# Layer 0 of a four-layer attention network: the first-layer sums of two points in one VectorE operation, with interleaved rows

## The chip, the cores and the metric

The kernel runs on one core of a Trainium2 chip. The number that counts is the device time of one execution in microseconds (us). Three executions of the kernel before took 3349.29, 3350.77 and 3352.3 us, median 3350.77 us.

A core has these engines, each with its own instruction queue: TensorE (PE in the profile, with its weight loads listed as PEld), VectorE (DVE), ScalarE (ACT), GpSimd (POOL) and SyncE (SP). In this kernel SP and POOL mostly issue DMA transfers. Engines wait for one another by semaphores. All arithmetic is in fp32.

## The reference, cut to what matters

Four layers run on x of shape (2, 512, 32, 32). The change lies in layer 0, deformable attention with 8 heads and 8 groups. Each group looks at 64 positions that are computed from the data, and the attention bias is a small network of the distance between each of the 1024 queries and each of these positions:

```python
pos = grid_q[:, :, None, :] - grid_kv[:, None, :, :]
bias = jnp.sign(pos) * jnp.log1p(jnp.abs(pos))
bias = jax.nn.relu(bias @ cpb_w1 + cpb_b1)      # 2 -> 128
bias = jax.nn.relu(bias @ cpb_w2 + cpb_b2)      # 128 -> 128
bias = (bias @ cpb_w3 + cpb_b3).reshape(b, GROUPS, H * W, Hd * Wd)
sim = jnp.einsum('bhid,bhjd->bhij', qh, kh) + bias
attn = jax.nn.softmax(sim, axis=-1)
```

Layers 1 to 3 are self-attention layers. The change doesn't touch them.

## The kernel before, in words

Layer 0 (function layer0) treats pairs of heads: t counts 8 of them, 2 images times 4 pairs. A pair has 128 positions, called points: 2 groups times 64. For each point the network's first layer is needed for 128 hidden channels (the partitions) and 1024 queries (32 rows y times 32 columns x).

**Tables.** The two distances of a point depend on x alone and on y alone. So offsets(t) computes, for each point, 32 numbers for x and 32 for y, and stores them to DRAM (slog_d, L471). load_tabs reads 16 points at a time back, spread over all partitions (L573), and scale_tab multiplies them by the channel's weight (VectorE for the first tables, L585; ScalarE after that, L587). What is left of the first layer is relu(tx[x] + ty[y]).

**first(p), L599.** One VectorE operation per point adds a row of 32 numbers, repeated over y, to a column of 32, repeated over x, and clips at zero: 1024 columns. It goes to one of eleven places (ring): three tiles of their own (named h1..., shown as h in the profile) and eight pieces of the buffer wa, which holds weights of layer 2 in the beginning and is otherwise free here.

**second, L616 and L625.** A step i takes four points. The 128 output channels of the second layer are cut into four parts of 32. For each part, eight matmuls (two halves of 512 queries times four points) fill one tile z: point k occupies partitions 32k to 32k+31, and its weights are 32 columns of cpb_w2, so that four matmuls with four different points run in the PE array side by side. In the trace an fp32 matmul is two records, so that a step has 64 of them. There are three z tiles in PSUM, which other small results share. ScalarE turns z into h2 with a relu and a bias per part (L625). Parts 1 and 3, the odd parts, go to the pool h2q, which has three buffers; part 2 goes to h2b (three buffers), part 0 to pieces of the buffer bridge or to h2j.

**joined, L630.** VectorE adds part 1 to part 0, and part 3 to part 2, with the sign that the third layer's weights need. GpSimd then issues DMA transfers that add the joined halves to each other and fold groups of partitions (L927 to L937), and SyncE copies some of them together (L931). third (L645) multiplies by the third layer's weights into sim, 20 steps late; scores (L653) adds the product of queries and keys.

**Order.** Everything in layer0 keeps, on each engine, the order in which the program writes it (in_order). The loop over i = 0 to 255 writes, for the parts k = 0 to 3 of a step: a call of first for point 4i + 7 + k (seven points are written ahead of the loop: AHEAD), the matmuls and the relu of a part, the joining of parts 3 and 2 of the step before at k = 1, and the joining of parts 1 and 0 at k = 3. Between them a chain of generators (behind) is advanced once at k = 1 and once at k = 3: finish(t) takes the softmax of the pair before, offsets(t+2) computes later positions (its small convolution: ScalarE products at L408, VectorE reductions at L414; then the small matmul po at L441), and samples(t+1) takes keys and values (kvbd at L534, wy, wx, shift, kq, values).

A place of the ring is rewritten as soon as PE has read it; the wait for this is VectorE's. In the same way ScalarE waits for a free buffer of h2q or h2b, and PE for a free z.

Before the loop PE multiplies weights of layer 2 together (folds, L135) while the first tables are made; small_fold ends with a VectorE operation at L855, after which VectorE's first sum is queued.

Of the kernel before, what the change touches and what calls it, by code (L numbers as in the profile page):

```python
# [79 lines left out]
def kernel(ctx: ExitStack, tc: tile.TileContext, a: dict, out: bass.AP):  # L80
# [111 lines left out]
    def layer0(l0, fold_d, t2_b, o2_b):  # L192
# [3 lines left out]
        two = l0.enter_context(tc.tile_pool(name="att2", bufs=2))  # L196
        vop = l0.enter_context(tc.tile_pool(name="att_vo", bufs=NPAIR))
        h2b = l0.enter_context(tc.tile_pool(name="att_h2b", bufs=3))
        h2q = l0.enter_context(tc.tile_pool(name="att_h2q", bufs=3))
        h2p = cycle([bridge[:, k, :] for k in range(6)])  # L200
        h2j = cycle([bridge[:, 6, :], bridge[:, 7, :], *(one.tile([P, HW], F32, name=f"h2j{k}") for k in range(2))])
        dram = l0.enter_context(tc.tile_pool(name="l0dram", bufs=1, space=DRAM))
# [30 lines left out]
        cpb_w2 = one.tile([P, P], F32, name="cpb_w2")  # L233
        nc.sync.dma_start(out=cpb_w2, in_=a["cpb_w2"])

        ring = [one.tile([P, HW], F32, name=f"h1{k}") for k in range(3)]
        ring += [qkv2.rearrange("p k n -> p (k n)")[:, k * HW : (k + 1) * HW] for k in range(6)]
        ring += [proj2.rearrange("p k n -> p (k n)")[:, k * HW : (k + 1) * HW] for k in range(2)]
        vb2 = one.tile([P, CC], F32, name="vb2")
        with nc.allow_non_contiguous_dma("512 numbers"):  # L240
            nc.sync.dma_start(out=vb2, in_=a["vb"][1].rearrange("(k p) -> p k", p=P))
# [7 lines left out]
        kvbd = [one.tile([P, P], F32, name=f"kvbd{i}") for i in range(2)]  # L249
        for w in actbd + kvbd:  # L250
            nc.gpsimd.memset(w, 0.0)
        ones = one.tile([P, P], F32, name="ones")
        nc.gpsimd.memset(ones, 1.0)


        qws = one.tile([P, NPAIR, P], F32, name="qws")
# [28 lines left out]
            nc.vector.tensor_tensor(dst, dst, src, ALU.max)  # L285

        def bias_weights():
            sort = h2b.tile([P, 7, P], F32, name="sort", tag="h2")
            row, below, w2t = [sort[:, k, :] for k in range(3)]
            perm = sort[:, 3:, :].rearrange("p b (r u) -> p b r u", u=32)  # L290
            few = one.tile([P, 28], F32, name="few")
            minus = few[:, 0:1]
            nc.vector.scalar_tensor_tensor(minus, cs("py", 0), 32.0, cs("px"), ALU.mult, ALU.add)
# [88 lines left out]
        def offsets(t):  # L382
# [85 lines left out]
            nc.scalar.activation(pos, pos, AF.Ln, bias=1.0)  # L468
            yield
            nc.vector.tensor_mul(pos, pos, sgn)  # L470
            nc.sync.dma_start(out=slog_d[t].rearrange("x p i -> p x i"), in_=pos)  # L471
            tables.add(t)

        tables = set()
# [10 lines left out]
        def samples(t):  # L485
# [22 lines left out]
                )  # L508
            nc.vector.tensor_mul(wsum[:, 2:3], wsum[:, 0:1], wsum[:, 1:2])
            yield  # L510
            wx = one.tile([P, P], F32, name="wx")
            nc.scalar.activation(wx, gpb[:, 0, :], AF.Abs, bias=cs("px"))
            nc.scalar.activation(wx, wx, AF.Relu, bias=1.0, scale=-1.0)
            wy = one.tile([P, 8, P], F32, name="wy", tag="wy")
# [11 lines left out]
            accumulate(pk[:, 0, :], [(xt[:, k, :], wy[:, k, :]) for k in range(8)])  # L526
            accumulate(pk[:, 1, :], [(wsum[:, 2:3].to_broadcast([P, P]), ident)])
            yield
            shift = one.tile([P, P], F32, name="shift")
# [12 lines left out]
            kq = one.tile([P, P], F32, name="kq")  # L542
# [3 lines left out]
            values = one.tile([P, P], F32, name="values")  # L546
            nc.scalar.copy(values, pkv[:, 1, :])
            yield
            pvo = zt([P, HW], "pvo")
# [39 lines left out]
        def first(p):  # L589

            chunk, point = divmod(p, 16)
            if point == 0:
                tabs_of.pop(chunk - 1, None)
                if chunk + 1 < NT * NCH:
                    load_tabs(chunk + 1)
            tx, ty = tabs_of[chunk]
            h1 = ring[p % len(ring)]

            nc.vector._custom_dve(  # L599
                TENSOR_ADD_SAT,  # L600
                out=h1.rearrange("p (y x) -> p y x", x=W),
                in0=tx[:, point, :].unsqueeze(1).to_broadcast([P, H, W]),
                in1=ty[:, point, :].unsqueeze(2).to_broadcast([P, H, W]),
                s0=float(np.finfo(np.float32).max),
                s1=0.0,
            )
            return h1

        def second(i, h1s, part):

            z = zt([P, HW], "z")
            lo = BLOCK[part]
            for half in range(2):
                n = slice(half * HALF, (half + 1) * HALF)
                for point in range(4):
                    nc.tensor.matmul(  # L616
                        z[point * 32 : point * 32 + 32, n],
                        cpb_w2[:, lo : lo + 32],
                        h1s[point][:, n],
                        start=True,  # L620
                        stop=True,
                    )
            ring = h2q if part % 2 else h2b if part else h2j if i % (4 if i < LAST else 2) else h2p
            h2 = ring.tile([P, HW], F32, name="h2", tag="h2") if ring in (h2q, h2b) else next(ring)
            nc.scalar.activation(h2, z, AF.Relu, bias=b2h[:, part : part + 1])  # L625
            return h2
# [30 lines left out]
        def finish(t, sim):  # L657

            b, pr = divmod(t, NPAIR)
            if pr == 0:  # L660
                aTs[b] = one.tile([P, NPAIR, HW], F32, name="aT")
            simb = one.tile([P, HW], F32, name="simb", tag="simb")
            nc.scalar.activation(simb, sim, AF.Identity, bias=simbias[t])
            yield
            table(AF.Exp)
            pt = zt([P, 8, P], "pt")
            for i in range(8):
                nc.tensor.transpose(pt[:, i, :], simb[:, i * P : (i + 1) * P], ident)
# [5 lines left out]
            at = one.tile([P, 8, P], F32, name="at", tag="simb")  # L674
# [12 lines left out]
            yield  # L687
            pa = zt([P, 8, P], "pa")
            for i in range(8):
                nc.tensor.transpose(pa[:, i, :], at[:, i, :], ident)  # L690
            nc.scalar.copy(aTs[b][:, pr, :], pa.rearrange("p i j -> p (i j)"))
            yield
            if pr < NPAIR - 1:
                return
            for m in range(CC):
                pp = zt([P, HW], "pp")
                project_out(pp, b, m, range(NPAIR))
                add_out(b, m, slice(0, HW), pp)
                yield
# [17 lines left out]
        def finish_last(sim, eights, fours, right_sums, left_sums):  # L717
# [7 lines left out]
            simb = one.tile([P, HW], F32, name="simb", tag="simb")  # L725
# [158 lines left out]
        steps = NT * NR  # L884
        h1s, parts, joins, sim, w1s = {}, {}, {}, None, None
        behind = chain(small_steps, offsets(1), samples(0))
        AHEAD = 7

        for p in range(AHEAD):
            h1s[p] = first(p)  # L890
        late_loads()
        for i in range(steps):
            for k, part in enumerate((1, 0, 3, 2)):
                if i % 4 == 1 and k % 2 == 0 and i // 4 + 1 in tabs_of:
                    scale_tab(i // 4 + 1, k // 2)
                p = 4 * i + AHEAD + k
                if p < 4 * steps:
                    h1s[p] = first(p)
                due = i - 20
                if k == 1 and 0 <= due < LAST and due % 16 == 0:  # L900
                    t, r = divmod(due, NR)
# [1370 lines left out]
```

## Time and profile before

| what | value |
| --- | --- |
| median of three executions | 3350.77 us |
| profiled execution | 3353.46 us |
| its span, first to last instruction | 3351.7 us |
| mean granted TensorE clock | 0.998 |
| PE busy | 3323.8 us (99%) |
| DVE busy | 2673.0 us (80%) |
| ACT busy | 1805.5 us (54%) |
| POOL busy | 676.7 us (20%) |
| first z matmul of the loop | at 59.6 us |
| last z matmul of the loop | at 1981.6 us |
| L599, first layer's sums | 1024 times, 1216 ns each |
| L630, joinings | 512 times, 1276 to 1277 ns each |

The profile is of one execution. Busy time is the time in which an engine had an instruction under way; matmuls are pipelined, so that four z matmuls which start together are recorded as some 593 ns each, while the next four start about 427 ns after them. A row of a group gives line, engine, operation, output and inputs, how often, then busy time and the mean in ns. In the timeline and the lists of waits, "<-" names what ended an idle time. "issue" means that nothing which the profile shows was waited for. L599 is line 599 of the kernel before; the same statement has another number in the kernel after (L599 becomes L603, L616 becomes L623, L625 becomes L632, L630 becomes L637).

### The profile page before, as it was taken

The page shows a single profiled execution, that of the slowest core. Times are in us where ns is not written, and L with a number is a line of the kernel's source. Part 1 is how long each engine was busy: PE and PEld are TensorE (multiplying, and loading weights), DVE is VectorE, ACT ScalarE, POOL GpSimd, SP SyncE. Part 2 cuts the span into 40 slices and gives each one's busy share as a digit, 9 for nine tenths or more (in the row PEclk, how much of TensorE's full clock was granted, in tenths as well). Part 3 has the DMA queues.
Part 4 walks back from the last instruction along what each step waited for, and adds up shares of the span by engine and source line. Part 5 has one row for each costly group of instructions (what it writes and reads, how often), then busy time and mean ns, then how long its engine had stood idle before and what let it go on. Part 6 is the DMA issues. An engine that isn't in the chain of part 4 may idle for free.

```text
span 3351.7 us, 61808 instructions
## 1 busy us (share of the span) xinstructions
PE 3323.8 (99%) x24813; PEld 1611.7 (48%) x24813; DVE 2673.0 (80%) x3540; ACT 1805.5 (54%) x2774; POOL 676.7 (20%) x804
## 2 busy tenths in 40 slices
PE   9999999999999999999999999999999999999999
PEld 4333333332333332333333339999953443687777
DVE  6999999999999799999999976455446465665556
ACT  4866877877877577877877652122136245122221
POOL 0333333333333233333333310000000000000000
PEclk9999999999999999999999999999999999999999
DMA  5778787787787577787787751000100000000111
GB/s 166 157 161 166 153 168 156 152 166 153 158 167 155 103 162 155 159 169 152 158 166 157 161 135 58 14 8 14 52 0 14 26 29 20 7 7 3 30 32 36
DMA packets 142488, 343.97 MB, mean 103 GB/s; under 512 B 36464, under 2 KB 51440, under 8 KB 141424
## 3 DMA queue, kind: packets, MB, share of 16 engines
q0 software_dynamic: 68400, 231.26, 36.5%
q1 hardware_dynamic: 72496, 103.95, 10.7%
q8 instruction: 197, 3.23, 0.4%
q10 hardware_dynamic: 1296, 4.72, 0.4%
q14 instruction: 99, 0.81, 0.1%
HBM read 71.46 MB, written 10.83 MB: 25 GB/s over the span
## 4 chain that ended last, share of the span: by engine, by line
PE 82%; DVE 9%; issue 5%; DMA 2%; ACT 1%; POOL 1%; DVEq 0%; SPq 0%; POOLq 0%; ACTq 0%
PE z L616 38%; PE pma L135 6%; PE pw L1435 6%; PE pmb L135 5%; PE pmv L1435 4%; PE score L1614 3%; PE pv L1626 3%; DVE wa L599 3%; PE pm L1435 3%; PE score L1435 3%; PE pmt L1435 1%; PE ppr L1435 1%; DVE h L599 1%; DMA bridge<-h 1%; DVE bridge L630 1%
## 5 line engine op out<-in xcount | busy, mean ns | idle before, releaser
L616 PE MATMUL z<-wa,cpb_w 128*32 128x512 f32 x11904 | 1779.2, 593 | 5.8 <-ACT h L625 3.7
L625 ACT ACTIVATE h<-z,b2h 128x1024 f32<-128x1024 f32 x768 | 851.3, 1114 | 347.9 <-PE z L616 310.6
L616 PE MATMUL z<-h,cpb_w 128*32 128x512 f32 x4480 | 983.2, 593 | 1.6 <-ACT h L625 1.6
L616 PEld LDWEIGHTS z<-wa,cpb_w 128*32 128x32 f32 x11904 | 497.2, 110 | 888.2 <-issue 778.1
L599 DVE CUSTOM_DVE_ANT_1 wa<-tab,tab 128x1024 f32<-128x1024 f32 x744 | 878.1, 1216 | 1.3 <-PE z L616 1.1
L616 PEld LDWEIGHTS z<-h,cpb_w 128*32 128x32 f32 x4480 | 256.6, 110 | 328.6 <-issue 292.1
L599 DVE CUSTOM_DVE_ANT_1 h<-tab,tab 128x1024 f32<-128x1024 f32 x280 | 332.9, 1216 | 2.3 <-PE z L616 2.2
L630 DVE SCALAR_TENSOR_TENSOR h<-h,turn,h 128x1024 f32<-128x1024 f32 x256 | 326.8, 1276 | 4.3 <-ACT h L625 4.3
L625 ACT ACTIVATE bridge<-z,b2h 128x1024 f32<-128x1024 f32 x162 | 180.8, 1116 | 121.4 <-PE z L616 119.0
L927 POOL DMA_DIRECT2D bridge<-bridge x150 | 127.6, 850 | 547.2 <-DMA bridge<-h 510.5
L630 DVE SCALAR_TENSOR_TENSOR bridge<-bridge,turn,h 128x1024 f32<-128x1024 f32 x162 | 206.8, 1277 | 4.2 <-ACT bridge L625 4.2
L934 POOL DMA_DIRECT2D bridge<-h x161 | 163.4, 1015 | 213.2 <-DVE h L630 123.6
L1278 ACT COPY p<-pma 128x128 f32<-128x128 f32 x80 | 21.3, 266 | 334.7 <-PE pma L135 334.7
L1270 DVE TENSOR_TENSOR upper<-pma,p 128x256 f32<-128x256 f32 x80 | 33.7, 422 | 178.6 <-ACT p L1278 178.5
L1615 ACT ACTIVATE p<-score 128x512 f32<-128x512 f32 x256 | 130.0, 624 | 81.2 <-PE score L1614 79.6
L927 POOL DMA_DIRECT2D h2j<-h2j x90 | 76.2, 847 | 323.0 <-DMA h2j<-h 293.6
L1647 DVE TENSOR_TENSOR acc<-acc,p 128x1024 f32<-128x1024 f32 x96 | 111.0, 1217 | 19.4 <-ACT p L1615 19.3
L625 ACT ACTIVATE h2j<-z,b2h 128x1024 f32<-128x1024 f32 x94 | 105.0, 1117 | 37.9 <-PE z L616 37.3
L1614 PE MATMUL score<-q,k 64*128 64x512 f32 x512 | 120.7, 604 | 1.1 <-DVE gm L1191 1.1
L630 DVE SCALAR_TENSOR_TENSOR h2j<-h2j,turn,h 128x1024 f32<-128x1024 f32 x94 | 120.0, 1276 | 0.0
L1626 PE MATMUL pv<-p,vT 128*64 128x512 f32 x512 | 116.5, 598 | 0.0
L937 POOL DMA_DIRECT2D bridge<-h2j x90 | 111.9, 1244 | 2.6 <-issue 1.8
(458 smaller groups left out, 4379.8 us busy)
## 6 DMA issues: line engine op xcount, KB each, us to landing
bridge<-h POOLq DMA_DIRECT2D x161, 512.0 KB, 5.5
h2j<-h POOLq DMA_DIRECT2D x94, 512.0 KB, 5.9
bridge<-bridge POOLq DMA_DIRECT2D x159, 256.0 KB, 3.9
tab<-slog_d SPq DMA_DIRECT2D x128, 256.0 KB, 4.6
h2j<-h2j POOLq DMA_DIRECT2D x90, 256.0 KB, 3.2
bridge<-bridge POOLq DMA_DIRECT2D x150, 128.0 KB, 5.4
bridge<-bridge SPq DMA_DIRECT2D x90, 128.0 KB, 3.7
bridge<-h2j SPq DMA_DIRECT2D x90, 128.0 KB, 3.6
```

The source lines that it names most:

```text
L135: nc.tensor.matmul(pm, w, m, start=(k == 0), stop=(k == len(pairs) - 1))
L599: nc.vector._custom_dve(TENSOR_ADD_SAT, out=h1.rearrange("p (y x) -> p y x", x=W), in0=tx[:, point, :].unsqueeze(1).to_broadcast([P, H, W] ...
L616: nc.tensor.matmul(z[point * 32 : point * 32 + 32, n], cpb_w2[:, lo : lo + 32], h1s[point][:, n], start=True, stop=True,)
L625: nc.scalar.activation(h2, z, AF.Relu, bias=b2h[:, part : part + 1])
L630: nc.vector.scalar_tensor_tensor(h2, h2, turn[:, part // 2 : part // 2 + 1], parts.pop(part + 1), ALU.mult, ALU.add)
L927: nc.gpsimd.dma_start(out=own[0:P:2], in_=own[1:P:2], accum_op=ALU.add)
L934: nc.gpsimd.dma_start(out=joins[i - 1], in_=other, accum_op=ALU.add)
L937: nc.gpsimd.dma_start(out=joins[i - 3 - j][j:P:4], in_=joins.pop(i - 3)[2:P:4], accum_op=ALU.add)
L1435: nc.tensor.matmul(out, stationary(l, k), moving(r, k), start=start and k == 0, stop=k == nk - 1, skip_group_check=not start,)
L1614: nc.tensor.matmul(sc, ks[m][r, s * P : (s + 1) * P], qs[m][r, n], start=True, stop=True)
L1615: nc.scalar.activation(p[:, part], sc, AF.Exp, scale=64 ** -0.5)
L1626: nc.tensor.matmul(pv[half][part * 64 : part * 64 + 64], vt[s % 4][:, lo : lo + 64], lps[s, half][:, part, :], start=(s == 0), stop=(s == 7),)
```

## The change

first(p) now makes the sums of two points, p and p + 1, in one operation of 2048 columns. Their rows are interleaved in the result: row y of the first point, then row y of the second, then row y + 1 of the first. Six double places make up the ring, room for twelve points, and eight points are written ahead of the loop. In a step the operation is written at k = 0 and k = 2. The matmuls of second read a point out of this: 16 runs of 32 words, 32 words apart.

For the operand ty the pair's 64 numbers have to lie as (y, point). The table in DRAM is stored in that order: the x half of slog_d is one DMA as before, the y half is two DMAs in which each number is a run of its own, 2048 numbers each.

The odd parts' pool h2q gets a fourth buffer. To make room, ones becomes a part of the tile sort and is set by VectorE, and some tiles share a buffer: simb and at with wy, wx with values, shift with kq.

```diff
-        h2q = l0.enter_context(tc.tile_pool(name="att_h2q", bufs=3))
+        h2q = l0.enter_context(tc.tile_pool(name="att_h2q", bufs=4))
...
-        ring = [one.tile([P, HW], F32, name=f"h1{k}") for k in range(3)]
-        ring += [qkv2.rearrange("p k n -> p (k n)")[:, k * HW : (k + 1) * HW] for k in range(6)]
-        ring += [proj2.rearrange("p k n -> p (k n)")[:, k * HW : (k + 1) * HW] for k in range(2)]
+        ring = [one.tile([P, 2 * HW], F32, name=f"h1{k}") for k in range(2)]
+        ring += [qkv2.rearrange("p k n -> p (k n)")[:, k * 2 * HW : (k + 1) * 2 * HW] for k in range(3)]
+        ring.append(proj2.rearrange("p k n -> p (k n)"))
...
-        ones = one.tile([P, P], F32, name="ones")
-        nc.gpsimd.memset(ones, 1.0)
...
-            sort = h2b.tile([P, 7, P], F32, name="sort", tag="h2")
+            sort = h2b.tile([P, 8, P], F32, name="sort", tag="h2")
+            ones = sort[:, 7, :]
+            nc.vector.memset(ones, 1.0)
...
-            nc.sync.dma_start(out=slog_d[t].rearrange("x p i -> p x i"), in_=pos)
+            nc.sync.dma_start(out=slog_d[t, 0], in_=pos[:, 0, :])
+            pairs = slog_d[t, 1].rearrange("(a k) i -> a (k i)", k=2).rearrange("a (i k) -> k a i", k=2)
+            with nc.allow_non_contiguous_dma("4096 numbers"):
+                for k in range(2):
+                    nc.sync.dma_start(out=pairs[k], in_=pos[k:P:2, 1, :])
...
-            wx = one.tile([P, P], F32, name="wx")
+            wx = one.tile([P, P], F32, name="wx", tag="values")
...
-            tx, ty = tabs_of[chunk]
-            h1 = ring[p % len(ring)]
+            tx, ty = [tab[:, point : point + 2, :] for tab in tabs_of[chunk]]
+            h1 = ring[p // 2 % len(ring)].rearrange("p (y k x) -> p y k x", k=2, x=W)
 
             nc.vector._custom_dve(
                 TENSOR_ADD_SAT,
-                out=h1.rearrange("p (y x) -> p y x", x=W),
-                in0=tx[:, point, :].unsqueeze(1).to_broadcast([P, H, W]),
-                in1=ty[:, point, :].unsqueeze(2).to_broadcast([P, H, W]),
+                out=h1,
+                in0=tx.unsqueeze(1).to_broadcast([P, H, 2, W]),
+                in1=ty.rearrange("p k y -> p (k y)")
+                .rearrange("p (y k) -> p y k", k=2)
+                .unsqueeze(3)
+                .to_broadcast([P, H, 2, W]),
                 s0=float(np.finfo(np.float32).max),
                 s1=0.0,
             )
-            return h1
+            return [h1[:, :, k, :] for k in range(2)]
...
-                        h1s[point][:, n],
+                        h1s[point][:, half * 16 : half * 16 + 16, :],
...
-            simb = one.tile([P, HW], F32, name="simb", tag="simb")
+            simb = one.tile([P, HW], F32, name="simb", tag="wy")
...
-        AHEAD = 7
-
-        for p in range(AHEAD):
-            h1s[p] = first(p)
+        AHEAD = 8
+
+        for p in range(0, AHEAD, 2):
+            h1s[p], h1s[p + 1] = first(p)
...
                 p = 4 * i + AHEAD + k
-                if p < 4 * steps:
-                    h1s[p] = first(p)
+                if p < 4 * steps and k % 2 == 0:
+                    h1s[p], h1s[p + 1] = first(p)
```

The shared buffers of at, shift, kq and values are marked in the same way as those of wx and simb, by a tag.

More of the change, by code (lines that the diff above doesn't have):

```diff
@@ L287, in bias_weights @@
         def bias_weights():
[L288 removed]
+            sort = h2b.tile([P, 8, P], F32, name="sort", tag="h2")
+            ones = sort[:, 7, :]
+            nc.vector.memset(ones, 1.0)
             row, below, w2t = [sort[:, k, :] for k in range(3)]
[L290 removed]
+            perm = sort[:, 3:7, :].rearrange("p b (r u) -> p b r u", u=32)
             few = one.tile([P, 28], F32, name="few")
@@ L528, in samples @@
             yield
-            shift = one.tile([P, P], F32, name="shift")
+            shift = one.tile([P, P], F32, name="shift", tag="kq")
             nc.scalar.mul(shift, pk[:, 1, :], col("bn1_b", pr))
@@ L541, in samples @@
             nc.tensor.matmul(pkv[:, 1, :], bd["vw"][:, pr, :], kv, start=True, stop=True)
-            kq = one.tile([P, P], F32, name="kq")
+            kq = one.tile([P, P], F32, name="kq", tag="kq")
             nc.scalar.copy(kq, pkv[:, 0, :])
@@ L545, in samples @@
             nc.scalar.mul(kqs[t], pkv[:, 0, :], s1q[:, pr : pr + 1])
-            values = one.tile([P, P], F32, name="values")
+            values = one.tile([P, P], F32, name="values", tag="values")
             nc.scalar.copy(values, pkv[:, 1, :])
@@ L673, in finish @@
             yield
-            at = one.tile([P, 8, P], F32, name="at", tag="simb")
+            at = one.tile([P, 8, P], F32, name="at", tag="wy")
             atv = at.rearrange("p i (g j) -> p (i g) j", j=NJ)
@@ L724, in finish_last @@
             project_out(pps[0], b, 0, range(2))
-            simb = one.tile([P, HW], F32, name="simb", tag="simb")
+            simb = one.tile([P, HW], F32, name="simb", tag="wy")
             for half, n in enumerate(halves):
```

## The prediction

> **What bounds the kernel now.** I read the table of busy time by stretch first, over eight stretches of the attention loop of layer 0, then the list of waits inside that loop, then the timeline around one repeated wait, then the rows of single groups for prices. The table (microseconds, PE, PEld, DVE, ACT, POOL busy) has these rows; the last line sums 70 to 1980 us:
>
> ```profile
> 300.00:540.00 240.00, 238.94 (x2168) 75.63 (x2164) 234.53 (x215) 182.02 (x253) 83.84 (x97) 1.00 0.78 159
> ...
> 1020.00:1260.00 240.00, 239.58 (x1972) 77.02 (x1968) 212.67 (x196) 162.00 (x233) 74.82 (x87) 1.00 0.68 139
> ...
> sum 1910.00, PE 1901.06 PEld 597.72 DVE 1839.46 ACT 1405.93 POOL 650.69; mean PE 237.63 PEld 74.71 DVE 229.93 ACT 175.74 POOL 81.34
> ```
>
> Two engines are nearly full: DVE has 71 us free in 1910, PE 9. So TensorE is the bound, and whatever VectorE saves is worth at most those 9 us. That PE's busy time is real work and not slow work shows in the chain that ended last, asked over 100 to 470 us:
>
> ```profile
> 210.64 109.87 PE z L616 x1024
> ...
> 428.48 1.21 DVE bridge L630
> 429.77 1.12 ACT h L625
> 430.93 8.79 PE z L616 x80
> ```
>
> 1024 records in 109.87 us are 256 groups of four column blocks at 0.429 us. A step of the loop has 64 records: 6.87 us of PE. DVE's step is two of each half: sums of two points 2.35 us, one joining (L630). Starts of such pairs lie 3.47 us apart (426.12 and 429.59 below), so 6.94 us per step, 0.07 more than PE, before any other VectorE work. DVE falls behind, and catches up only where PE has other matmuls.
>
> The 9 us of PE are these waits (total, times, longest), and below them ScalarE's waits for VectorE in the same stretch:
>
> ```profile
> PE z L616 <- ACT h L625: 5.3, 10, 0.6
> PE z L616 <- DVE kvbd L534: 2.1, 2, 1.6
> PE sim L645 <- DMA bridge<-bridge: 1.5, 2, 1.3
> ...
> ACT h L625 <- DVE h L630: 9.0, 8, 1.3
> ACT h L625 <- DVE bridge L630: 7.0, 6, 1.4
> ```
>
> The timeline (start, duration) shows how one of the first kind arises:
>
> ```profile
> 426.12 2.35 DVE L599 CUSTOM_DVE_ANT_1 wa<-tab,tab 128x1024 f32<-128x1024 f32 x2
> ...
> 428.39 1.28 DVE L630 SCALAR_TENSOR_TENSOR bridge<-bridge,turn,h 128x1024 f32<-128x1024 f32 x1
> ...
> 429.77 2.12 ACT L625 ACTIVATE h<-z,b2h 128x1024 f32<-128x1024 f32 x2 [1.36 <-DVE bridge L630]
> ...
> 430.93 0.64 PE L616 MATMUL z<-wa,cpb_w 128*32 128x512 f32 x4 [0.52 <-ACT h L625]
> ```
>
> ScalarE waits 1.36 us until the late joining frees one of three odd-part buffers; then PE waits for ScalarE. This recurs at 668, 908, 1411 and 1649 us. The other five waits for ACT h (455, 693, 932, 1436, 1674 us) follow a run of ScalarE's own small operations with no VectorE wait ahead of them.
>
> **The change part by part.**
>
> *The paired sum.* 1024 operations of 1024 columns become 512 of 2048. One takes 1216 ns. VectorE rows of 512 and 1024 columns (L1717 at 692, L1647 at 1217 ns) give 1.03 ns a column, so a pair should take 1216 + 1024 x 1.03 = 2.27 us against 2.35: 0.08 saved, 512 times, 41 us of VectorE. DVE's step becomes 6.94 - 2 x 0.08 = 6.78 us, below PE's 6.87. Both operands keep their kind, runs of 64 repeated and words repeated 32 times, for which the present runs of 32 already cost nothing over a plain 1024-column operation (1216 against 1217 ns). On the path the 41 us are worth nothing themselves: PE's matmuls cover them.
>
> *Twelve points, eight ahead, a fourth odd buffer.* The last point of a step was written in the step before it; now it is a full step earlier. Counted from the release of its place, VectorE had 6.87 - 1.2 = 5.7 us of room for it; now the second pair ends 2.27 + 1.2 + 2.27 = 5.7 us after the release and is read two PE steps after it, so the room is 13.7 - 5.7 = 8.0 us. The fourth buffer lets ScalarE run two quarter steps, 3.4 us, further ahead of the joining; the waits of 1.36 us end inside that. By starts of matmuls each of the five stops costs 0.72 us over the normal spacing: 5 x 0.72 = 3.6 us, all taken as gone. What comes late next is ScalarE itself: its five own runs stay, 5 x 0.55 = 2.7 us. The waits for kvbd (1.63 and 0.42 us) are VectorE lag: by 177 us it has done some 34 pairs, 2.7 us earlier, less one sum more before the loop (1.1 us); I take 1.5 us of the 2.1. The waits of L645 for a DMA (1.29 and 0.21 us) follow from late joinings and from queues; bounds 0 and 1.5, I take 0.5.
>
> *TensorE reads every second row.* Its moving operand becomes 16 runs of 32 words with as many skipped. Bounds come from three rows; in the first the code reads single words four apart, in the second two runs of 256, in the third 512 in one run:
>
> ```profile
> L1752 PE MATMUL pb<-proj,vb x8: 1047/1090/1339, 2621.5 to 2622.7; 128*32 128x512 f32 x8
> ...
> L1898 PE MATMUL den<-acc,ones x16: 592/604/617, 2940.4 to 3119.5; 128*32 128x512 f32 x16
> ...
> L616 PE MATMUL z<-wa,cpb_w x11904: 589/592/617, 59.6 to 1981.6; 128*32 128x512 f32 x199
> ```
>
> At worst a hop costs what it costs between single words, (1090 - 592) / 512 = 0.97 ns: 15 hops in 4096 groups are 60 us. At best nothing; a gain is excluded, since the same columns stream. Runs of 32 are nearer to runs of 256 than to single words, and L343, whose moving operand also has runs of 32, takes 275 ns like its contiguous neighbours of 128 columns. I take 0.
>
> The Trainium skill, page "Advanced Engine Details and Errata", section "Memory Cachelines", speaks against the edit in one line, that any non-contiguous access pattern slows matmuls significantly, and for it in another, that SBUF needs two hits on a 16-byte line. The first stands under PSUM, and by it the sum would move to the 60 us end; by the second it stays at 0, and L1752, one hit a line, is the slow row under both.
>
> *The y table written interleaved.* One store of 32 KB (L471) becomes one of 16 KB and two of 2048 single numbers, eight times; SP issues three instructions for one (0.36 to 1.3 us each) and is held at the y load until they land; the folded weights' stores queue behind. The first table is on the path. Its rows:
>
> ```profile
> 44.18 0.48 DVE L585 TENSOR_SCALAR tab<-tab,pc 128x512 f32<-128x512 f32 x1 [0.33 <-DMA tab<-slog_d]
> ...
> 52.70 0.16 DVE L855 TENSOR_TENSOR o_b<-pb,pc 128x4 f32<-128x4 f32 x1 [8.04 <-PE pb L135]
> ...
> 59.57 0.63 PE L616 MATMUL z<-h,cpb_w 128*32 128x512 f32 x3
> ...
> vb<-in_vb SPq DMA_DIRECT2D x1, 6.0 KB, 5.2
> ...
> d<-few SPq DMA_DIRECT2D x8, 2.0 KB, 1.4
> ```
>
> VectorE idles 8 us behind the table, and PE, busy with the folds until 59.6, needs two pairs (4.5 us) by then: the table may come by 55.1, 10.4 us late, for nothing. A load of 1536 single numbers lands in 5.2 us; all of it charged per number, 4096 take 13.9 us, 3.5 over the slack. The other end is nothing: a load of 512 such numbers took 5.1 us, so most is fixed. The far end is a store: 2 KB in 128 runs lands in 1.4 us (d<-few), all charged per run 45 us, 34 past the slack. I take 0, since the loads have runs of the same size. Later tables are needed some 100 us after their store; there the stores only share queue and engines with the join's transfers (L931, L937; median 3.7 and 5.7 us), bounds 0 and 1 us each, seven times; I take 0.5 in all.
>
> The page "DMA: Bandwidth & Descriptors", section "Specifications", says that below 512 B the engine does a read-modify-write. By that the stores would lie toward the far end; no row here stores single numbers to DRAM.
>
> *The rest*, all 0: ones is set by VectorE while it idles 2.79 us for prow at 15.7 us; shared buffers for wx and values, shift and kq, simb, at and wy follow one another in the same queues with matmuls between them. Cover gone, each would cost one ScalarE operation, about 1 us, per pair of heads.
>
> **Sum** against the profiled execution (3353.46 us, of which the span is 3351.7): -3.6 - 1.5 - 0.5 + 0.5 = -5.1, so 3348.4. That execution lies 2.7 us above the median 3350.77; on the median's scale 3345.7.
>
> **Rivals.**
>
> *All of PE's idle time goes* (30%): ScalarE's own runs are absorbed too, because it no longer enters them late. The list of waits allows 9 us: 3341.9. Against it: ScalarE had caught up (it waits 0.60 us for PE at 449.15) before the stop at 454.78.
>
> *Nothing goes* (8%): joinings stay late by something else, for instance if a pair takes 2.35 us or more. DVE's step is then again over PE's: 3351.
>
> *Slower: the hop is paid* (10%). Place: all 16384 matmuls of L616. Price: 4096 x 15 x c. From c = 0.08 ns the gain is gone, from 0.19 ns the kernel is slower by over 0.2%; at 0.97 ns 3406. Against it, L1898 and L343.
>
> *Slower: the single-number stores* (8%). At 45 us for the first table PE stands idle 34 us at 59.6 us: 3380; from 22 us to landing it decides. What is left (4%) is a joining chain that stops PE several times a head pair, 3358.
>
> **How the numbers follow.** 0.2% is 6.7 us, about what a measurement of this kernel can tell from no change. The forecast, a gain of 3 to 6.7 us, has 40%; with the 8% of nothing, same is 0.48; faster is 0.30; slower 0.10 + 0.08 + 0.04 = 0.22. The likeliest case's own range is 3344 to 3348. The range goes from 3340 (all idle time and two microseconds of spread between runs) to 3362, which takes in small prices of hop or store and leaves out their far ends.
>
> **What would show it.** L603, the sum's new line: 512 operations of 2.27 us; 2.43 or more would break the first step. The z matmuls stay at 592 ns, a group at 0.429 us; 600 or more shows the hop. ScalarE's waits for L637, the joining, fall from 21 us to under 5; PE's for ACT h from ten to five. DVE's idle time ahead of sums and joinings grows from about 12 to some 40 us, for it now waits for PE. The first z still starts near 59.6 us. I am wrong if PE's stops stay with VectorE 41 us lighter, or if z slows.

## The result, and the profile after

The kernel after takes 3440.78 us, median of six executions (3431.93 to 3446.95), against 3350.67 us of the kernel before on the same chip (six, 3348.89 to 3352.3). The ratio is 1.0269, with a 95% interval of 1.0257 to 1.0281: slower by 90 us. The profiled execution took 3440.16 us, its span is 3438.4 us, and its mean granted TensorE clock 0.988 where it was 0.998.

The page of the kernel after, busy time of each engine:

```profile
span 3438.4 us, 61019 instructions
...
PE 3347.4 (97%) x24813; PEld 1637.0 (48%) x24813; DVE 2640.2 (77%) x3029; ACT 1803.6 (52%) x2774; POOL 676.0 (20%) x803
```

VectorE is lighter by 33 us (2673.0 before; 41 were forecast), and yet the span is longer by 86.7 us; 83.3 of these are there when the last z matmul starts (2064.9 us, before 1981.6). The same table by stretch as in the prediction (PE, PEld, DVE, ACT, POOL busy, then granted clock, share of the DMA engines, GB/s), kernel after:

```profile
300.00:540.00 240.00, 231.15 (x2077) 80.48 (x2072) 220.14 (x144) 174.46 (x245) 81.16 (x94) 0.98 0.84 153
...
1020.00:1260.00 240.00, 235.08 (x1918) 74.00 (x1914) 202.63 (x129) 153.83 (x209) 75.25 (x88) 0.99 0.69 138
...
sum 1910.00, PE 1843.21 PEld 599.82 DVE 1739.71 ACT 1352.57 POOL 630.38; mean PE 230.40 PEld 74.98 DVE 217.46 ACT 169.07 POOL 78.80
```

PE now stands idle for 67 us of these 1910, where it was 9, and no other engine has taken over as the bound: VectorE has 170 us free, where it was 71. The list of waits of PE in the loop (total, times, longest), kernel after:

```profile
PE z L623 <- ACT h2j L632: 38.0, 6, 9.9
PE pk L135 <- ACT h2j L632: 11.1, 1, 11.1
PE sim L652 <- DMA bridge<-bridge: 7.2, 4, 4.4
PE z L623 <- ACT h L632: 5.6, 6, 2.9
PE z L623 <- DVE h L603: 4.6, 2, 4.4
PE pk L135 <- ACT bridge L632: 3.5, 1, 3.5
PE z L623 <- ACT bridge L632: 1.5, 2, 0.9
```

They add up to 71.5 us, 62.6 more than before. Few waits, and long: one or two for each pair of heads, the largest those that end at 183.9, 494.1, 743.8, 990.6, 1521.5 and 1767.4 us. The waits on which the forecast gain rested, two for kvbd and five behind the joining at the small matmul po, are gone; each of the six new stops costs more than all of those together. The timeline around the second stop, kernel after (start, duration):

```profile
465.92 0.33 SPq L471 DMA_DIRECT2D slog_d<-pos  x1
...
466.29 3.33 SPq L475 DMA_DIRECT2D slog_d<-pos  x2
...
469.15 0.86 POOL L934 DMA_DIRECT2D h2j<-h2j  x1 [3.56 <-DMA h2j<-h]
...
471.02 0.86 POOL L941 DMA_DIRECT2D bridge<-h  x1 [1.01 <-issue]
...
490.07 0.50 SPq L938 DMA_DIRECT2D bridge<-h2j  x1
...
491.51 0.86 POOL L934 DMA_DIRECT2D bridge<-bridge  x1 [18.78 <-DMA bridge<-h]
...
492.89 1.11 ACT L632 ACTIVATE h2j<-z,b2h 128x1024 f32<-128x1024 f32 x1 [11.02 <-issue]
...
494.05 2.79 PE L623 MATMUL z<-wa,cpb_w 128*32 128x512 f32 x12 [8.31 <-ACT h2j L632]
```

Read from the end. PE waits 8.3 us for a z tile that ScalarE has not emptied; ScalarE waits 11 us to write h2j ("issue" in the timeline; what it waits for follows from the kernel's order). Part 0 goes to four places in turn, two called h2j and two in bridge; out of the place that is due, SyncE's copy (L938) has still to read, and that copy goes out only at 490.07, since it needs the fold of h2j that GpSimd had issued at 469.15. GpSimd in turn waits 18.8 us for the transfer which it issued at 471.02. Both transfers were issued 3 to 5 us behind the two stores of single numbers (L475, issued in 466.29 to 469.62). The chain of work that ended last, asked over 480 to 500 us, says the same:

```profile
471.02 20.21 DMA bridge<-h
491.23 0.28 issue
491.51 0.56 POOL bridge L934
492.07 8.10 DMA bridge<-h
```

The median of such a transfer was 5.5 us before; this one takes 20.2. Now the stretches around it, as in the table above; first the kernel after, then the same part of the pair of heads in the kernel before:

```profile
470.00:484.00 14.00, 13.45 (x128) 3.91 (x124) 14.00 (x10) 10.67 (x20) 1.72 (x3) 1.00 1.57 29
484.00:494.00 10.00, 1.75 (x20) 0.26 (x8) 2.36 (x2) 1.11 (x2) 1.75 (x2) 0.70 0.89 151
494.00:499.00 5.00, 4.95 (x28) 1.24 (x32) 4.02 (x3) 4.07 (x4) 1.65 (x2) 0.57 1.08 256
```

```profile
452.00:466.00 14.00, 13.45 (x132) 3.94 (x128) 14.00 (x14) 12.24 (x25) 5.17 (x6) 1.00 0.94 224
```

For 14 us the DMA engines move 29 GB/s instead of 224, although packets are under way all the time (share 1.57: two queues' packets are open at once, SyncE's with a share of 0.78 and GpSimd's with 0.77). Nothing is lost on PE yet in this stretch (13.45 us busy in both); PE stops from 485.7 on. Then comes a second price: when PE starts again its granted clock is 0.57 in the mean of the next 5 us, and L623's longest matmul takes 1063 ns where it was 617. There are ten such stretches of half clock in the loop of after, 3.4 to 10.2 us each with the idle time in them, and none before. Counted by the starts in the trace, 39 groups of matmuls come some 0.85 us apart instead of 0.43, which is 17 us, and two runs of pk matmuls come 0.21 us apart instead of 0.11, which is 3.6 us. So 62.6 us of waits and some 21 us of slow clock make up the 83.3 us to within a few us; smaller terms on both sides I have not traced.

The page "TensorE: Matmul & The Clock Gate" of the Trainium skill, section "What's actually happening", says that an idle window of about 3.4 us halves TensorE's clock, until it has been busy for about as long. The granted clock of 0.57 behind a stop of 8.3 us agrees with it. The stop of 2.9 us that ends at 1285.8 us is shorter than that and still has half clock behind it (0.50 from 1286.8 to 1290.2 us); one of 2.2 us that ends at 2072.3 us has not (1.00).

The start of the loop, timeline of the kernel after:

```profile
37.89 18.16 SPq L577 DMA_DIRECT2D tab<-slog_d  x2
...
55.88 0.55 DVE L589 TENSOR_SCALAR tab<-tab,pc 128x512 f32<-128x512 f32 x1 [14.86 <-DMA tab<-slog_d]
...
59.12 0.49 DVE L589 TENSOR_SCALAR tab<-tab,pc 128x512 f32<-128x512 f32 x1 [2.69 <-DMA tab<-slog_d]
...
59.64 4.49 DVE L603 CUSTOM_DVE_ANT_1 h<-tab,tab 128x2048 f32<-128x2048 f32 x2
...
62.08 1.92 PE L623 MATMUL z<-h,cpb_w 128*32 128x512 f32 x4 [4.39 <-DVE h L603]
```

The first tables are ready at 59.6 instead of 44.7 us, 15 us later, and the first z comes 2.5 us later than before, after a stop of 4.4 us. Last, the rows of the two parts that were meant to change, kernel after (min, median and max in the second):

```profile
L603 DVE CUSTOM_DVE_ANT_1 wa<-tab,tab 128x2048 f32<-128x2048 f32 x340 | 776.6, 2285 | 3.0 <-PE z L623 2.6
```

```profile
L623 PE MATMUL z<-wa,cpb_w x10880: 592/592/1063, 75.1 to 2058.1; 128*32 128x512 f32 x198
```

A pair's sum takes 2.285 us, and a z matmul that reads every second row still takes 592 ns.

### The profile page after: what moved, and what is told of

Its sections match the earlier page's. It is cut to its first block, busy times and chain, and to the rows that moved or that the text cites. A ratio compares the mean times of both kernels' runs of the same rounds, so it can differ in the third digit from the quotient of the medians.

```text
span 3438.4 us, 61019 instructions
## 1 busy us (share of the span) xinstructions
PE 3347.4 (97%) x24813; PEld 1637.0 (48%) x24813; DVE 2640.2 (77%) x3029; ACT 1803.6 (52%) x2774; POOL 676.0 (20%) x803
## 4 chain that ended last, share of the span: by engine, by line
PE 73%; DMA 10%; DVE 7%; issue 7%; POOL 2%; ACT 1%; SPq 1%; DVEq 0%; POOLq 0%; ACTq 0%
PE z L623 32%; PE pma L135 6%; PE pw L1442 6%; DMA bridge<-h 5%; PE pmb L135 5%; PE pmv L1442 4%; PE score L1621 3%; PE pv L1633 3%; PE pm L1442 3%; PE score L1442 3%; DVE wa L603 2%; DMA bridge<-bridge 2%; PE ppr L1442 1%; DMA h2j<-h 1%; DVE h L637 1%
## 5 line engine op out<-in xcount | busy, mean ns | idle before, releaser
L623 PE MATMUL z<-wa,cpb_w 128*32 128x512 f32 x10880 | 1203.3, 596 | 33.1 <-ACT h2j L632 26.5
L603 DVE CUSTOM_DVE_ANT_1 wa<-tab,tab 128x2048 f32<-128x2048 f32 x340 | 776.6, 2285 | 3.0 <-PE z L623 2.6
L623 PEld LDWEIGHTS z<-wa,cpb_w 128*32 128x32 f32 x10880 | 364.3, 110 | 831.6 <-issue 697.2
L623 PE MATMUL z<-h,cpb_w 128*32 128x512 f32 x5504 | 618.5, 597 | 16.6 <-ACT h2j L632 11.4
L603 DVE CUSTOM_DVE_ANT_1 h<-tab,tab 128x2048 f32<-128x2048 f32 x172 | 392.9, 2285 | 1.4 <-PE z L623 1.2
L623 PEld LDWEIGHTS z<-h,cpb_w 128*32 128x32 f32 x5504 | 184.4, 110 | 422.3 <-issue 361.9
```

Of the source, the lines that this page charges most:

```text
L603: nc.vector._custom_dve(TENSOR_ADD_SAT, out=h1, in0=tx.unsqueeze(1).to_broadcast([P, H, 2, W]), in1=ty.rearrange("p k y -> p (k y)") .rear ...
L623: nc.tensor.matmul(z[point * 32 : point * 32 + 32, n], cpb_w2[:, lo : lo + 32], h1s[point][:, half * 16 : half * 16 + 16, :], start=True, ...
```

## Experiments: is it the stores?

Theory S: the two stores of 2048 single numbers hold up the transfers of the joining, and cost the 90 us. Rival P: something else in the change does, the ring of pairs, the matmuls' operand or the buffers that now share a place.

**The stores alone.** The kernel before, with the two stores of after and nothing else; a sum of one point reads its column two words apart.

```diff
-            nc.sync.dma_start(out=slog_d[t].rearrange("x p i -> p x i"), in_=pos)
+            nc.sync.dma_start(out=slog_d[t, 0], in_=pos[:, 0, :])
+            ...
+                for k in range(2):
+                    nc.sync.dma_start(out=pairs[k], in_=pos[k:P:2, 1, :])
...
```

> The kernel before with nothing changed but the store of the y table: two DMAs of 2048 single numbers, and the sum reads the column two words apart. Theory S: the whole loss is here, 3437 us (3425 to 3450), with the stops at the same places, and TensorE's clock halved after them. Rival P: within 0.2% of before, 3344 to 3357.

Measured: 3450.75 us (3447.52 to 3454.33) against 3349.93, ratio 1.03 (1.0283 to 1.0318). So the stores alone cost 101 us, somewhat more than S expected, and more than the whole change; by that the rest of the change would give about 10 us back. (The sum that reads words two apart takes 1218 ns against 1216, so it is not the sum.) The long waits of PE are there again:

```profile
PE z L624 <- ACT h2j L633: 47.3, 5, 13.4
PE z L624 <- ACT h L633: 21.7, 13, 8.8
```

**Half the numbers, waited for by nothing.** The kernel before, with one extra store of 2048 single numbers per pair of heads, into a DRAM tile that nobody reads. It tells whether the price is the traffic or the wait for the table.

```diff
+        spare_d = dram.tile([NT, P // 2, 64], F32, name="spare_d")
...
+            pairs = spare_d[t].rearrange("a (i k) -> k a i", k=2)
...
+                nc.sync.dma_start(out=pairs[0], in_=pos[0:P:2, 1, :])
```

> The kernel before with one spare DMA of 2048 single numbers per pair of heads to a scratch piece of DRAM, half of what the kernel after stores, and nothing that waits for it. Theory S in its plain form, that each number costs PE its share: 90 x 7/8 / 2 = 39 us, 3390 us. Theory S with room in the buffers (the engines are held for about half of 18 us, and the joining chain has some 7 us of room): 0 to 20 us, 3351 to 3371 us. Rival P: 3351 us.

Measured: 3394.97 us, ratio 1.0132 (1.0112 to 1.0152), 45 us more. Nothing waits for this store, so the price is what it does to the other transfers, and half of the numbers cost half.

**The same runs, not to DRAM.** Both stores of 2048 numbers, as extra work, from SBUF to a tile in SBUF.

```diff
+        spare_s = one.tile([P // 2, 64], F32, name="spare_s")
...
+            pairs = spare_s.rearrange("a (i k) -> k a i", k=2)
...
+                for k in range(2):
+                    nc.sync.dma_start(out=pairs[k], in_=pos[k:P:2, 1, :])
```

> The kernel before with two spare DMAs of 2048 single numbers per pair of heads that go from SBUF to SBUF, as many runs of as few bytes as in the kernel after, but no write to DRAM. If it is the number of runs that holds the engines: 3420 to 3440 us. If it is the writing of single numbers to DRAM: within 0.2% of before, 3344 to 3357 us.

Measured: 3350.11 us, ratio 1.0 (0.999 to 1.0009). In the 14 us behind the stores the DMA engines move 174 GB/s here, against 224 in the kernel before (table by stretch), so these stores are not free for them; but PE is as busy as before:

```profile
450.00:464.00 14.00, 13.45 (x132) 3.97 (x128) 14.00 (x14) 12.13 (x25) 4.32 (x5) 1.00 0.99 174
```

So it is not the number of runs, nor SyncE's time to issue them, nor the reading of single numbers from SBUF. It is writing them to DRAM, in this dense layout; the runs on other layouts follow below.

## Experiments: what is the rest of the change worth?

**The table stored whole.** The kernel after, with the store of before; the numbers of two points are interleaved later, in SBUF, by the operation that scales the y table anyway and now writes into a tile of its own. To make room, actbd, kvbd and the y table as it is loaded have one buffer each, and sums3 shares kq's.

```diff
-            nc.sync.dma_start(out=slog_d[t, 0], in_=pos[:, 0, :])
-            ...
+            nc.sync.dma_start(out=slog_d[t].rearrange("x p i -> p x i"), in_=pos)
...
+            if ax:
+                tabs_of[c][1] = two.tile([P, 16, 32], F32, name="taby")
+                dst = tabs_of[c][1].rearrange("p a y -> p (a y)").rearrange("p (a y k) -> p a k y", k=2, y=32)
+                tab = tab.rearrange("p (a k) y -> p a k y", k=2)
...
...
-                nc.scalar.activation(tab, tab, AF.Identity, bias=0.0 if ax else col("cpb_b1"), scale=w)
+                nc.scalar.activation(dst, tab, AF.Identity, bias=0.0 if ax else col("cpb_b1"), scale=w)
```

> The kernel after, with the table stored in one piece as before; the scaling that follows the load interleaves the y table into a tile of its own (room for it: one buffer each instead of two for actbd and kvbd, and sums3 shares kq's). The kernel before with single-number stores lost 100 us, the kernel after 90; so the rest of the change is worth 10 us: 3340 us (3336 to 3347). PE's waits in the loop fall from 9 us to under 4, z stays at 592 ns. Rival (the pairs help only where PE stands still for another reason, and give nothing without the stores): 3350 us within 0.2%. Rival (ScalarE's odd writes, up to 0.7 us a table, lengthen its runs): 3350 to 3357.

Measured: 3343.59 us (3340.41 to 3345.44) against 3350.78, ratio 0.998 (0.9971 to 0.9989): faster than the kernel before by 7.2 us. PE's waits in the loop:

```profile
PE z L624 <- ACT h L633: 3.0, 5, 0.6
PE sim L653 <- DMA bridge<-h: 2.1, 1, 2.1
```

The second lies behind the last z matmul (1968.5 us). In the loop 3.0 of the 8.9 us are left, five waits of 0.6 us that follow a run of ScalarE's own small operations, as at 451.4, 687.7 and 923.9 us. The pair's sum takes 2284 ns, the scaling of the y table 796 ns and that of the x table, still in place, 805: writing it interleaved costs nothing. More came out of the loop than these waits. From the first z matmul to the last it is 1909.8 us, where it was 1922.0, and the largest part of that lies in the matmuls of third, whose row took 35.6 us of busy time and 1.5 of waits before (first line, 60 to 1967 us) and takes 30.4 and no wait now (second line):

```profile
L645 PE MATMUL sim<-bridge,w 128*32 128x512 f32 x256 | 35.6, 594 | 1.5 <-DMA bridge<-bridge 1.5
```

```profile
L653 PE MATMUL sim<-bridge,w 128*32 128x512 f32 x256 | 30.4, 592 | 0.0
```

These 6.7 us, with 2.1 for kvbd and 2.3 for ACT h, are 11.1 of the 12.2; the wait of 2.1 us behind the last z takes some of it back.

**With three odd buffers.** The same kernel with the pool h2q as before.

```diff
-        h2q = l0.enter_context(tc.tile_pool(name="att_h2q", bufs=4))
+        h2q = l0.enter_context(tc.tile_pool(name="att_h2q", bufs=3))
```

> The run above with three odd-part buffers instead of four. If the waits for the joining at the small matmul po end by the lighter VectorE alone: as the run above, within 1 us. If they end by the fourth buffer, as the prediction has it: 3 to 4 us more than the run above, with PE's five waits of 0.52 us for ScalarE back.

Measured: 3343.41 us, ratio 0.998 (0.9971 to 0.9989), the same as with four. In the list of PE's waits the first line is the same too:

```profile
PE z L624 <- ACT h L633: 3.0, 5, 0.6
```

**The fourth odd buffer alone.** The kernel before with four buffers in h2q; simb and at move into wy's place for it.

> The kernel before with the fourth odd-part buffer alone (simb and at share wy's buffer to make room). If the buffer is what ends these five waits: 3 to 4 us less than before, 3346.5. If VectorE's lag shows up at the next buffer: within 1.5 us of before.

Measured: 3351.26 us, ratio 1.0 (0.9991 to 1.0009): no gain, where the interval leaves room for 3 us either way. Its list of PE's waits, and its row for the matmuls of third (60 to 1967 us), show why:

```profile
PE sim L645 <- DMA bridge<-bridge: 2.8, 4, 1.5
PE z L616 <- ACT h L625: 2.7, 5, 0.5
PE z L616 <- DVE kvbd L534: 2.1, 2, 1.7
```

```profile
L645 PE MATMUL sim<-bridge,w 128*32 128x512 f32 x256 | 37.7, 595 | 2.9 <-DMA bridge<-bridge 2.8
```

The buffer does take away the five waits at po (ten become five, 5.3 us become 2.7), but the joinings come no earlier, and third pays for it: its matmuls take 37.7 us and 2.9 of waits, where they took 35.6 and 1.5. New waits for these transfers stand at 676.2, 1419.8 and 1657.7 us, some 8 us behind the places of three of the stops that are gone. Gain and loss, 2.6 and 3.5 us, cancel within what the runs can tell. In the two runs with the paired sums the waits for these transfers inside the loop are gone, with or without the buffer.

## Experiments: what makes such a store dear?

All of these are the kernel before with extra stores that nothing reads, as in the run with half the numbers, but in other layouts. In the code shown, the loop over k and lines that repeat are left out at the dots. Theory A: each number is dear by itself. Theory B: it is dear to write single numbers close to one another.

**Each number 64 bytes from the next:** 4096 numbers, spread over 256 KB.

```diff
+        spare_d = dram.tile([NT, P // 2, 64, 16], F32, name="spare_d")
...
+            pairs = spare_d[t].rearrange("a (i k) s -> k a i s", k=2)
...
+                    nc.sync.dma_start(out=pairs[k, :, :, 0], in_=pos[k:P:2, 1, :])
```

> The kernel before with two spare stores of 2048 single numbers each per pair of heads, every number 64 bytes from the next instead of 8 or 4, and nothing that waits for them. If it is each partial write to DRAM that is dear, wherever it goes: 3430 to 3450 us. If it is partial writes close together that wait for one another: clearly less, 3350 to 3390 us.

**The same 16 KB in another order,** so that numbers which one transfer stores one after the other lie far apart: 512 bytes by the code below (the expectation says 256, which is the distance between the two transfers).

```diff
+            pairs = spare_d[t].rearrange("a b -> (a b)").rearrange("(i k a) -> k a i", k=2, a=P // 2)
...
```

> The kernel before with two spare stores of 2048 single numbers per pair of heads into 16 KB, as in the kernel after, but laid out the other way round: numbers that one transfer writes one after the other lie 256 bytes apart, and 64 bytes are filled by 16 different rows. If consecutive writes into the same 64 bytes wait for one another: clearly less than the loss of 100 us, 3350 to 3375 us. If it is that all of them go to the same small piece of DRAM: 3430 to 3450 us.

**Runs of two numbers:** 2 x 1024 runs of 8 bytes, which fill the same 16 KB.

```diff
+            pairs = spare_d[t].rearrange("a (i k j) -> k a i j", k=2, j=2)
...
+                    nc.sync.dma_start(out=pairs[k], in_=pos[k:P:2, 1, :].rearrange("p (i j) -> p i j", j=2))
```

> The kernel before with two spare stores of 1024 runs of two numbers (8 bytes) each per pair of heads, dense in 16 KB. If each partial write has its price, half of it: 3400 us (as the spare store of 2048 single numbers, 3395). If it is the bytes: 3440 us. If runs of 8 bytes are free: 3351 us.

**32 and 16 bytes apart:** as the first, with 8 and 4 words per number instead of 16.

> The kernel before with the two spare stores of 2048 single numbers each, each number 32 bytes from the next (each of the two DMAs writes every 64 bytes). If the collisions are between writes of one DMA into the same 64 bytes: as with 64 bytes apart, 3355 us. If the small piece of DRAM matters, something between 3355 and 3440 us.

> The kernel before with the two spare stores of 2048 single numbers each, each number 16 bytes from the next, so that two numbers share 32 bytes, in 64 KB per pair of heads. At 32 bytes apart (128 KB) the cost was 6 us, dense (16 KB) some 90 to 100. If writes that share 32 bytes collide: most of the loss or half of it, 3390 to 3450 us. If the size of the piece is what matters: near the wide ones, 3355 to 3375 us.

**Two numbers in the same 32 bytes, 128 KB:** they lie 16 bytes apart, and the next two 64 bytes on.

```diff
+        spare_d = dram.tile([NT, P // 2, 32, 16], F32, name="spare_d")
...
+                    nc.sync.dma_start(out=spare_d[t, :, :, 4 * k], in_=pos[k:P:2, 1, :])
```

> The kernel before with the two spare stores of 2048 single numbers each in 128 KB per pair of heads, as wide as at 32 bytes apart (3357 us), but the two numbers of a row lie 16 bytes apart in the same 32 bytes, as at 16 bytes apart in 64 KB (3401 us). If writes that share 32 bytes collide: 3390 to 3405 us. If the size of the piece is what matters: 3352 to 3362 us.

What was measured, each against the kernel before on its own chip:

| extra stores per pair of heads | runs in 64 bytes | piece of DRAM | median, us | ratio (95%) | us more |
| --- | --- | --- | --- | --- | --- |
| 4096 numbers, 64 bytes apart | 1 | 256 KB | 3355.26 | 1.001 (1.0001 to 1.002) | 4.5 |
| 4096 numbers, 32 bytes apart | 2 | 128 KB | 3356.85 | 1.0017 (1.0008 to 1.0027) | 5.7 |
| 4096 numbers, two in the same 32 bytes | 2 | 128 KB | 3357.64 | 1.0016 (1.0007 to 1.0026) | 6.5 |
| 4096 numbers, 16 bytes apart | 4 | 64 KB | 3401.42 | 1.015 (1.0133 to 1.0167) | 50 |
| 2048 numbers, 8 bytes apart | 8 | 16 KB | 3394.97 | 1.0132 (1.0112 to 1.0152) | 45 |
| 2048 runs of two numbers | 8 | 16 KB | 3395.04 | 1.013 (1.0112 to 1.0149) | 44 |
| 4096 numbers, other order | 16 | 16 KB | 3431.97 | 1.0241 (1.0224 to 1.0258) | 81 |

Theory A falls: the same 4096 runs of 4 bytes cost 4.5 us or 81, by where they lie. The price goes by runs and not by bytes (2048 runs of 4 and of 8 bytes cost the same), and writing neighbours far apart in time takes little from it: numbers stored one after the other 512 bytes apart still cost 81 us when they fill the same 16 KB in the end. The 20 us between this and the run with the stores alone (101) can be the order or the tables that wait there; no run separates the two. That the harm comes from two numbers in the same 32 bytes falls as well: with two of them there the cost is 6.5 us, as with none (5.7). The jump lies between two runs in 64 bytes and four. Between eight and sixteen runs in 64 bytes, both in 16 KB, the price of a run is nearly the same (22 us a thousand, and 20). In all the other steps the density and the size of the piece go together, so which of the two makes the price, many writes to a line or many writes to a small piece, stays open.

The table by stretch shows the same step in the 14 us behind the stores. Numbers 64 bytes apart, then 16 bytes apart:

```profile
450.00:464.00 14.00, 13.45 (x128) 3.89 (x124) 14.00 (x14) 12.52 (x25) 4.32 (x5) 1.00 0.97 174
```

```profile
457.00:471.00 14.00, 13.45 (x128) 3.91 (x124) 14.00 (x14) 11.94 (x25) 2.57 (x3) 1.00 1.24 91
```

174 GB/s at a share of 0.97, as with the stores that stay in SBUF, against 91 at 1.24. The cheap store is still not free: beside its 4.5 us, PE's list has a new wait of 1.2 us for h2j, and L650's for the joining's transfers are 3.7 us (L645's were 1.5).

## Why the prediction was wrong, point by point

**The step that failed is the price of the single-number stores in the loop.** The prediction bounded it by "0 and 1 us each, seven times" and took 0.5 us in all. Measured, two such stores hold the joining's transfers for some 18 us, and one pair of heads then costs 10 to 13 us: 101 us for eight pairs where the tables wait for them, 81 with the other order and nothing that waits. That the stores share the queue and the engines with the joining's transfers the prediction saw; what it had at nearly nothing was how long they hold them. The rows of before show single numbers only in loads, and for the first table the prediction went by "the loads have runs of the same size". A load was the wrong neighbour, and so would a copy inside SBUF have been (ratio 1.0 measured). The far end that the prediction did work out, 45 us for one store charged by its runs, was used for the first table alone. The bound for the loop had no row of a store behind it; charged like the first table, 7 x 45 us, it would have reached to 315 us, and the chance of slower would have grown with it.

The rival "the single-number stores" named the right part of the change but the wrong place. It had the harm in the wait for the first table, with PE idle for 34 us; the table came 15 us late and PE stood for 4.4. What happened instead is close to the last 4%, "a joining chain that stops PE several times a head pair", priced at 7 us of the median and worth more than ten times as much.

**The first table.** Taken as 0, with a slack of 10.4 us. The nearer bound, by number, said 13.9 us to landing and 3.5 over the slack; measured are 15 us and a stop of 4.4, so the choice of 0 was wrong. That the bound came out close is partly luck: it was worked out from loads, and it is the stores that are slow.

**The pair's sum** was nearly right: 2.27 us predicted, 2.285 measured, 512 times; VectorE is lighter by 33 us and not 41. **The strided operand** was right: 592 ns as before, and in the run with the table stored whole the longest is 618, where it was 617. One of the prediction's two supports was weaker than it says: L343 has two records, of 275 and 356 ns, and only the first agrees with its neighbours. Of the two lines of the Trainium skill ("Advanced Engine Details and Errata", "Memory Cachelines"), the one on SBUF, two hits on a 16-byte line, agrees with these 592 ns; the one on non-contiguous patterns stands under PSUM, and this operand lies in SBUF.

**The gain of the rest** was nearly right as a number: -5.6 without the stores by the prediction's terms, -7.2 measured (interval 3.7 to 9.7 by the ratio). Its parts were not, and that is luck. In the list of waits it is 5.9 us less of idle PE in the loop: the five waits at po, the 2.1 us for kvbd (of which 1.5 were taken) and the 1.5 us of L645 (of which 0.5). The matmuls of third gave 6.7 us with their busy time, and some was lost again behind the loop. So PE's busy time was not all real work, as the prediction had it, and the 9 us of waits were no ceiling. ScalarE's own five waits stay at 3.0 us, as forecast, so the rival "all of PE's idle time goes" falls.

**The fourth buffer** had 3.6 us of this to its name, together with the earlier sums. Alone it gains nothing that can be measured, and without it the same 7 us are gained. Either ends the waits at po, the buffer alone or the pairs without it; but only with the pairs do the joinings come in time for third. Whether that is the lighter sum or the eight points ahead in a ring of twelve, no run separates. ScalarE's waits for the joining did not fall "to under 5" either: with the table stored whole they are 11.1 us in 15 waits, while PE's waits for ACT h did go from ten to five.

**VectorE's idle time** ahead of sums and joinings was to grow from 12 to some 40 us. With the table stored whole it is 14.6. Some of the time shows elsewhere, ahead of small operations that wait for ScalarE and PE (mx 29.4 to 34.7, kvbd 0.2 to 6.2, simbias 7.6 to 11.9 us).

The page "DMA: Bandwidth & Descriptors", section "Specifications", with its read-modify-write below 512 B, pointed the right way, but gives no price: the same 4-byte runs cost between 4.5 and 81 us here. The same page, section "Why small descriptors are slow (HBM only)", excepts transfers inside SBUF, and the run that stayed in SBUF agrees (ratio 1.0). The reasons given there, a fixed overhead per packet and the descriptors' own bytes, can't be all, since the number of runs is the same in the cheapest and the dearest of these stores.

## What to carry to other kernels

Price a store by where and how densely its runs land and by what else is on the DMA engines, not by its bytes or its own deadline: 16 KB written to DRAM word by word held up the other transfers of this kernel for nearly 20 us. If data has to be interleaved, do it where an engine writes it anyway; here the scaling of the table did it for nothing, and the change then gave its 7 us. And where a bound has no row of the same direction and the same memory behind it, leave its far end in the range.

## What the runs showed of the hardware

- A thousand runs of 4 or 8 bytes to DRAM, eight times in the kernel, cost some 20 us when eight or sixteen of them share 64 bytes, 12 with four and 1.1 to 1.6 with one or two (the last column above by the number of runs). Inside SBUF the same runs cost no time that can be measured (ratio 1.0, 0.999 to 1.0009).
- While the dear stores are under way the DMA engines look busier than ever (share 1.57) and move an eighth of the bytes (29 against 224 GB/s). Here the share of busy time of the DMA engines is therefore no measure of their work.
- In the kernel after, each of the ten stops of PE in the loop that lasted 2.9 us or more had half-clock matmuls behind it, some 21 us in all on top of the stops; the stops of 2.2 us and less had none.
